# Batches 0 and 1 combined, and two groups' attention scores begun, beside the rear expert tiles

## The chip, the cores and the metric

The kernel runs on one NeuronCore of one Trainium2 chip, in fp32 throughout. The metric is the device time of one execution in microseconds; the median of three runs is given. Engines are named as in the profile: PE (TensorE), PEld (its weight loads), DVE (VectorE), ACT (ScalarE), POOL (GpSimd), SP (SyncE, which only issues DMAs here).

## The reference, cut to what matters

Four batches (B) of 512 tokens (S) with 256 features (D) go through four blocks. Each block adds its output to x.

```python
x = x + L0_xattn(layernorm(x), ctx, ctx)       # attention over log-ratios, then an MLP of 1024
x = x + L0_ffn(layernorm(x))                   # 8 experts of 1024, every token goes to its best two
x = x + L1_xattn(layernorm(x), ctx, ctx)       # 16 heads of 16 features
x = x + L1_ffn(x)                              # 8 experts of 512, every token goes to its best one

# L0_ffn, for all tokens t = (x @ W_in + b_in) of all four batches:
probs = softmax(t @ W_gate + b_gate);  topv, topi = top_k(probs, 2);  topv /= sum(topv)
out = (sum over the two: topv * (relu(t @ W1[e] + b1[e]) @ W2[e] + b2[e])) @ W_out + b_out

# L1_xattn, per batch and head:
scores = (q @ k.T) / sqrt(16);  ctx = softmax(scores) @ v;  out = ctx @ Wo + bo

# L1_ffn: one expert per token
out = max(gates) * (gelu(x @ W1[e] + b1[e]) @ W2[e] + b2[e])
```

## The kernel before, in words

**Layer 0, dense part.** Attention and MLP of the four batches run interleaved. `choose` picks each token's two experts and `Dispatch.send` scatters the token's row, with its share and its number, into an array `sent` in DRAM, where each expert has a region of its own. Keys and values of layer 1 need only the context; `remember` computes them here and stores them to DRAM.

**Layer 0, expert tiles.** A tile is 256 rows of one expert (TT). Which expert and which row a tile has is known only on the chip. `leave` and `plan` compute it on DVE in small operations (8 to 184 elements per partition) from the counts of rows; SP reads expert and row with `value_load`. One tile, of the expert with most rows, is worked early inside the dense part (`work`). Then `Dispatch.tiles` runs 19 tiles (`usual`) without a branch, and behind a branch on the true count (L625, L626) the few that may be left, which these inputs do not need.

One tile is: `load` (rows from `sent`, w1, w2, b1, b2 by SP), `turned` (4 transposes, `psIn`), `hide` (8 chunks of `mid` with their PSUM tiles `pm`, evicted by ACT and DVE in turn, L638 and L636), `give` (2 tiles `po`; ACT makes y = b2*share at L598, DVE adds po*share at L601) and `scatter` (POOL writes y's rows to `came` by an indirect DMA, L523). The next tile's `load` and `turned` stand between a tile's `hide` and its `give`. In layer 1 (`direct`) a tile has 4 chunks, x is gathered by POOL (L506), DVE adds it at L605, and POOL scatters to the output.

**The order of tiles.** The tiles that hold batch 0's rows come first: `send.zero` keeps the counts after batch 0, and `leave` makes from it how many tiles of each expert stand in front (`front`). After at most 11 tiles (FRONT) batch 0 is complete in `came`. So `bring(0, ..)` loads its two picks, `combine(0)` adds them and multiplies by W_out (L1105), `prepare(0)` normalizes and makes the queries `qc` (L1125), in steps of three after each tile, by `also(i)`. `place(0)` copies the queries by 16 small DMAs of SP into `qT`, where each head has 32 partitions. `early` clears `kT`, `qT` and `va` on POOL (`places`) and fetches batch 0's keys and values.

**Layer 1, attention.** A group is four heads of one batch; there are 16 groups. Scores are made twice: by query (`sc`, for the row maximum, DVE reduces it into `nm` at L1218) and by key (`scT`, ACT takes the exponential at L1215). `put_greatest` transposes `nm` and adds the negated maximum into row 0 of each head in `qT`. Scores by query run two groups ahead (AHEAD = 2), so the loop starts at group -2: groups -2 and -1 only have scores by query, four heads at a time. Later a quartet is two `sc` and two `scT` on four row groups of PE. `weigh` multiplies with the values (`av`, L1232), `divide` normalizes. Between quartets, two lanes (`fore`, `back_`) fill in the combining and preparing of batches 1 to 3, `finish` and `choose`. PE's order is written by hand here; in the expert tiles all engines' orders come from the framework's planner.

```python
            fore.work += [waiting(4), combines[1], prepares[1], placed(1), prepares[2], prepares[3]]
            back_.work += [waiting(5), combines[2], waiting(6), combines[3]]
            for i in range(-AHEAD, groups):
```

**Layer 1, expert tiles.** Three tiles are worked early (`work`, `soon`), then 8 tiles by `tiles`.

Of the kernel before, what the change touches and what calls it, by code (L numbers as in the profile page):

```python
# [43 lines left out]
def xattn_ffn_kernel(ctx: ExitStack, tc: tile.TileContext, a: dict, out: bass.AP):  # L44
# [240 lines left out]
    class Dispatch:  # L285


        def __init__(self, layer, pool, seen, n, func, b1_all):
            self.layer, self.pool, self.group = layer, pool, f"send{layer}"
            self.n, self.func, self.b1_all = n, func, b1_all  # L290
            self.w1_all, self.w2_all, self.b2_all = (a[f"L{layer}_ffn_{x}"] for x in ("W1", "W2", "b2"))
            self.kept = []
            self.zero = None
            self.seen_pool = seen
            self.seen = seen.tile([P, NT + 1, NE], F32, tag="seen0", name="seen0")
            nc.vector.memset(self.seen[:, 0, :], 0.0)
# [82 lines left out]
        def leave(self):  # L379
# [13 lines left out]

            front = least
            past_used = small.tile([P, NE, CAP // TT], F32, tag="past_used", name="past_used", bufs=1)
            nc.vector.tensor_tensor(past_used, over(used, CAP // TT), full, ALU.add)
            if self.zero is not None:
                more = small.tile([P, NE, CAP // TT], F32, tag="more", name="more", bufs=1)
                front = small.tile([P, NE], F32, tag="front", name="front")
                nc.vector.tensor_tensor(more, over(self.zero, CAP // TT), past_used, ALU.is_gt)  # L400
                nc.vector.tensor_reduce(front, more, AX.X, ALU.add)
                nc.vector.tensor_tensor(front, front, least, ALU.max)

            behind = small.tile([P, NE + 1], F32, tag="behind", name="behind")
            nc.vector.memset(behind[:, NE : NE + 1], float(NE * CAP))
            nc.vector.scalar_tensor_tensor(behind[:, 0:NE], front, float(TT), start[:, 0:NE], ALU.mult, ALU.add)
            nc.vector.tensor_copy(start[:, NE : NE + 1], behind[:, 0:1])
            self.stride = pool.tile([P, NE], F32, tag="stride", name="stride")
            nc.vector.tensor_tensor(self.stride, behind[:, 1 : NE + 1], behind[:, 0:NE], ALU.subtract)
            self.full = pool.tile([P, NE, CAP // TT], F32, tag="full_i", name="full_i")  # L410
            nc.vector.scalar_tensor_tensor(
                self.full, over(front, CAP // TT), float(TT), past_used, ALU.mult, ALU.add
            )

            self.first = pool.tile([P, TILES0], F32, tag="first_i", name="first_i")
            if self.zero is not None:
                end = small.tile([P, NE], F32, tag="end", name="end")
                nc.vector.tensor_tensor_scan(end, ones[:, 0:NE], front, 0.0, ALU.mult, ALU.add)
                jump = small.tile([P, NE], F32, tag="jump", name="jump")
                nc.vector.tensor_tensor(jump, start[:, 1 : NE + 1], start[:, 0:NE], ALU.subtract)  # L420
                nc.vector.scalar_tensor_tensor(jump, front, -float(TT), jump, ALU.mult, ALU.add)
                past = small.tile([P, TILES0, NE], F32, tag="past", name="past", bufs=1)
                nc.vector.tensor_tensor(past, number, end.unsqueeze(1).to_broadcast([P, TILES0, NE]), ALU.is_ge)
                self.e_front = pool.tile([P, TILES0], F32, tag="e_front", name="e_front")
                nc.vector.tensor_reduce(self.e_front, past, AX.X, ALU.add)
                nc.vector.scalar_tensor_tensor(
                    self.e_front, self.e_front, float(NE), self.e_front, ALU.is_lt, ALU.mult
                )
                nc.vector.tensor_tensor(past, past, jump.unsqueeze(1).to_broadcast([P, TILES0, NE]), ALU.mult)
                nc.vector.tensor_reduce(self.first, past, AX.X, ALU.add)  # L430
                nc.vector.scalar_tensor_tensor(
                    self.first, number[:, :, 0], float(TT), self.first, ALU.mult, ALU.add
                )
                nc.vector.tensor_scalar(self.first, self.first, start[:, 0:1], None, ALU.add)
                self.in_front = pool.tile([P, 1], F32, tag="in_front", name="in_front")
                nc.vector.tensor_copy(self.in_front, end[:, NE - 1 : NE])
            else:
                nc.vector.tensor_scalar(self.first, number[:, :, 0], float(TT), start[:, 0:1], ALU.mult, ALU.add)

            self.row_0 = pool.tile([P, 1], I32, tag="row_0", name="row_0")  # L440
            nc.vector.tensor_copy(self.row_0, start[:, 0:1])

        def plan(self):
# [11 lines left out]
            nc.vector.tensor_scalar(end, end, 1.0 if self.zero is None else self.in_front, None, ALU.add)  # L455
# [13 lines left out]
            if self.zero is None:  # L469
# [93 lines left out]
        def tiles(self, n_tiles, usual, tp, midp, pm_pool, po_pool, also):  # L563
# [30 lines left out]
            def give(rows, w2, added, mid):  # L594
                b2, x = added
                y = tp.tile([P, TT // P, D], F32, tag="y", name="y", bufs=2 if x is None else 3)
                for u in range(TT // P):
                    nc.scalar.mul(y[:, u, :], b2, rows[:, u, D:TO])  # L598

                def take(u, po):  # L600
                    nc.vector.scalar_tensor_tensor(  # L601
                        y[:, u, :], po, rows[:, u, D:TO], y[:, u, :], ALU.mult, ALU.add
                    )
                    if x is not None:
                        nc.vector.tensor_tensor(y[:, u, :], y[:, u, :], x[:, u, :], ALU.add)  # L605
                    self.scatter(rows, u, y)

                together(project(mid, w2, po_pool, take))

            def run(first, last):  # L610
# [3 lines left out]
                for i in range(first, last):  # L614
                    mid = midp.tile([P, n // P, TT], F32, tag="mid", name="mid")
                    together(hide(mid, w1, inT, b1, self.func, pm_pool))
# [4 lines left out]
                    give(*now)  # L621
                    also(i)

            run(0, usual)
# [53 lines left out]
    with tc.tile_pool(name="l0a", bufs=2) as lp, tc.tile_pool(name="l0tmp", bufs=2) as tp, tc.tile_pool(  # L678
# [279 lines left out]
        for b in range(B):  # L958
# [9 lines left out]
            if b < B - 1:  # L968
# [3 lines left out]
                if b == 1:  # L972
                    n, _ = send.counted("n0")
                    send.zero = fp0.tile([P, NE], F32, tag="zero", name="zero")
                    nc.vector.tensor_copy(send.zero, n[:, 0, :])
# [12 lines left out]
            with tc.manual_schedule(engines={mybir.EngineType.PE}):  # L988
# [24 lines left out]
                together(second)  # L1013
                send.plan()
# [12 lines left out]
    for i in range(2):  # L1027
        nms.append(heads.tile([P, NT, 4, 32], F32, tag=f"nm{i}", name="nm"))
        nc.gpsimd.memset(nms[i], 0.0)

    def places(pool):
# [3 lines left out]
        qT = pool.tile([P, NG, S], F32, tag=f"qT{i}", name=f"qT{i}")  # L1035
        va = pool.tile([P, NT, HEADS, 32], F32, tag=f"va{i}", name=f"va{i}")
        kTs.append(kT)
        qTs.append(qT)
        vas.append(va)
        for w in (kT, qT, va):  # L1040
            tc.keep_in_program_order(nc.gpsimd.memset(w, 0.0))
            yield
# [40 lines left out]
    def bring(b, k, pool, engine):  # L1083

        if b not in ys:
            tag = f"y{b}" if b == 0 else "w1" if b % 2 else "w2"
# [22 lines left out]
    def prepare(b, pool):  # L1109
# [4 lines left out]
        qc = qcs[b] = pool.tile([P, NC, S], F32, tag="qc", name="qc", bufs=1 if b == 0 else 2)  # L1114
# [15 lines left out]
    def place(b):  # L1130

        qT = qTs[b % 2]
        if b:
            together(fetch(b))
        if b > 1:
            for r in range(4):
                nc.gpsimd.memset(qT[32 * r : 32 * r + 1, :, :], 0.0)
        for hd in range(HEADS):
            g, r = divmod(hd, 4)
            m, at = divmod(hd * DH, P)  # L1140
            tc.keep_in_program_order(
                nc.sync.dma_start(qT[32 * r + 1 : 32 * r + 1 + DH, g, :], qcs[b][at : at + DH, m, :])
            )
# [3 lines left out]
    FRONT = (2 * S + NE * (TT - 1)) // TT  # L1147
# [35 lines left out]
    with tc.tile_pool(name="l1a", bufs=2) as lp, tc.tile_pool(name="l1s", bufs=1) as sp, tc.tile_pool(  # L1183
# [149 lines left out]
        def waiting(n):  # L1333
            yield n
# [182 lines left out]
```

## Time and profile before

| | us |
|---|---|
| median of 3 runs (1004.81 to 1006.11) | 1006.1 |
| the profiled execution | 1005.28 |
| its span, first to last instruction | 1003.5 |
| PE busy | 950.3 |
| DVE busy | 518.5 |
| ACT busy | 362.4 |
| POOL busy | 291.4 |
| mean granted TensorE clock | 0.987 |

Places in the span: the 19 tiles of layer 0 take PE from 303.65 to 585.05, the first mixed quartet of the attention starts at 612.65, and layer 1's 8 tiles take PE from 930.3 to 993.2.

How to read it: lines give start and length in us, the engine, the line of the kernel, the operation with its result and operands, and in square brackets how long the engine was idle before and what ended that. A matmul of fp32 appears as two records. A time given from one start to the next is more telling than a record's own length, since matmuls overlap. L12 is line 12 of the kernel before.

### The profile page before, as it was taken

Reading aid. Unit: us, or ns where it says so; the run is one execution under the profiler, and the core shown is the slowest. Engines: PE = TensorE matmul, PEld = TensorE weight load, DVE = VectorE, ACT = ScalarE, POOL = GpSimd, SP = SyncE. Lnnn points to the kernel's source line nnn. Section 1 sums busy time; section 2 is a strip of 40 time slices with the busy share of each in tenths; the row PEclk is TensorE's granted clock in tenths of the full one; section 3 lists DMA queues with packets and bytes.
Section 4 is the critical chain, followed back from the end, with each engine's and each line's share of the span. In section 5 each row is a group of like instructions: output and inputs, shape, how many; then the busy total and the mean of one; then the engine's idle time right before and its main releaser. Section 6 shows DMA issues by size and latency. Waiting matters only on the chain. (4 is left out here: it accounts for less than half of the span.)

```text
span 1003.5 us, 14228 instructions
## 1 busy us (share of the span) xinstructions
PE 950.3 (95%) x4885; PEld 640.2 (64%) x4885; DVE 518.5 (52%) x1401; ACT 362.4 (36%) x703; POOL 291.4 (29%) x333
## 2 busy tenths in 40 slices
PE   6999899899999999999999989999999999997995
PEld 4656667575778888888888854333333433356784
DVE  6674665566752222222323258576687777724232
ACT  5654232213212111211121204655656555573331
POOL 4341233244241312211112155315023221133453
PEclk9999999999999999999999999999999999999998
DMA  8599999944244566557654441101011103045672
GB/s 278 195 257 250 247 243 241 243 118 153 86 143 142 187 216 209 174 179 259 233 160 161 130 148 33 27 12 47 2 38 48 43 1 105 32 115 154 211 225 73
DMA packets 113233, 146.05 MB, mean 146 GB/s; under 512 B 14580, under 2 KB 94717, under 8 KB 113152
## 3 DMA queue, kind: packets, MB, share of 16 engines
q1 hardware_dynamic: 106112, 128.19, 45.3%
q0 software_dynamic: 6624, 15.80, 4.8%
q8 instruction: 43, 0.70, 0.3%
q10 hardware_dynamic: 416, 1.05, 0.3%
q14 instruction: 38, 0.31, 0.1%
HBM read 86.71 MB, written 58.80 MB: 145 GB/s over the span
## 5 line engine op out<-in xcount | busy, mean ns | idle before, releaser
L1218 DVE TENSOR_REDUCE nm<-sc 128x1 f32<-128x512 f32 x256 | 165.2, 683 | 60.9 <-PE scT L1211 57.3
L1215 ACT ACTIVATE ex<-scT 128x512 f32<-128x512 f32 x256 | 138.4, 596 | 96.2 <-PE scT L1211 95.8
L634 PE MATMUL pm<-inT,w 128*128 128x256 f32 x736 | 166.3, 382 | 2.5 <-ACT mid L638 2.1
L647 PE MATMUL po<-w,mid 128*128 128x256 f32 x736 | 163.3, 379 | 0.0
L1211 PE MATMUL sc<-kT,qT 32*128 32x512 f32 x512 | 154.5, 650 | 3.7 <-DVEq L626 1.6
L634 PEld LDWEIGHTS pm<-inT,w 128*128 128x128 f32 x736 | 139.9, 191 | 23.6 <-ACT mid L638 4.0
L647 PEld LDWEIGHTS po<-w,mid 128*128 128x128 f32 x736 | 138.1, 190 | 17.8
L1211 PE MATMUL scT<-qT,kT 32*128 32x512 f32 x512 | 148.5, 639 | 0.9 <-ACT ex L1215 0.9
L523 POOL DMA_INDIRECT came<-y,rows x38 | 37.4, 985 | 224.1 <-DVE y L601 224.1
L244 POOL TENSOR_TENSOR rstd<-var,halved 128x4 f32<-128x4 f32 (+1 forms) x32 | 28.1, 882 | 228.9 <-DVE var L243 224.4
L601 DVE SCALAR_TENSOR_TENSOR y<-po,rows,y 128x256 f32<-128x256 f32 x54 | 26.1, 484 | 130.5 <-PE po L647 120.6
L638 ACT ACTIVATE mid<-pm,b 128x256 f32<-128x256 f32 x108 | 49.9, 471 | 109.2 <-PE pm L634 93.5
L1211 PEld LDWEIGHTS sc<-kT,qT 32*128 32x128 f32 x512 | 49.8, 185 | 59.9 <-DVE nm L1218 36.9
L636 DVE TENSOR_SCALAR mid<-pm,b 128x256 f32<-128x256 f32 x76 | 36.7, 483 | 95.0 <-PE pm L634 95.0
L598 ACT ACTIVATE y<-b,rows 128x256 f32<-128x256 f32 x54 | 24.5, 500 | 159.2 <-DMA b<-in_L_ffn_b 133.0
L339 POOL DMA_INDIRECT sent<-rows,slot x48 | 47.3, 985 | 102.8 <-DVE slot L336 62.3
L1232 PE MATMUL av<-ex,va 128*32 128x512 f32 x512 | 68.6, 605 | 0.0
L763 PE MATMUL pm<-hT,w 128*128 128x512 f32 x128 | 62.2, 611 | 0.5 <-DVE hT L676 0.5
L769 PE MATMUL po<-w,mid 128*128 128x256 f32 x256 | 59.2, 381 | 0.0
L769 PEld LDWEIGHTS po<-w,mid 128*128 128x128 f32 x256 | 47.9, 190 | 9.1 <-issue 3.1
L1211 PEld LDWEIGHTS scT<-qT,kT 32*128 32x128 f32 x512 | 45.6, 183 | 6.0 <-issue 4.2
L1232 PEld LDWEIGHTS av<-ex,va 128*32 128x32 f32 x512 | 10.2, 108 | 48.2 <-issue 36.4
(312 smaller groups left out, 1257.6 us busy)
## 6 DMA issues: line engine op xcount, KB each, us to landing
w<-in_L_ffn_W SPq DMA_DIRECT2D x40, 1024.0 KB, 7.2
sent<-nowhere SPq DMA_DIRECT2D x32, 1161.0 KB, 20.4
w<-in_L_ffn_W SPq DMA_DIRECT2D x22, 512.0 KB, 4.3
rows<-sent SPq DMA_DIRECT2D x27, 258.0 KB, 4.9
b<-in_L_ffn_b SPq DMA_DIRECT2D x28, 128.0 KB, 6.6
y<-came SPq DMA_DIRECT2D x6, 512.0 KB, 8.7
x<-in_x SPq DMA_DIRECT2D x4, 512.0 KB, 5.1
c<-in_ctx SPq DMA_DIRECT2D x4, 512.0 KB, 5.6
```

The costliest lines, as they stand in the source:

```text
L339: i = nc.gpsimd.indirect_dma_start(out=sent[self.layer][:, :], out_offset=bass.IndirectOffsetOnAxis(ap=slot[:, t - tts[0], k : k + 1], axi ...
L523: i = nc.gpsimd.indirect_dma_start(out=came[self.layer][:, :], out_offset=bass.IndirectOffsetOnAxis(ap=rows[:, u, TO:ROW].bitcast(I32), ax ...
L634: nc.tensor.matmul(pm, w1[:, c, ts(k, P)], inT[:, c, :], start=c == 0, stop=c == NC - 1)
L636: nc.vector.tensor_scalar(mid[:, k, :], pm, bias[:, k : k + 1], 0.0, ALU.add, ALU.max)
L638: nc.scalar.activation(mid[:, k, :], pm, func, bias=bias[:, k : k + 1])
L647: nc.tensor.matmul(po, mid[:, k, ts(t, P)], w2[:, k, :], start=k == 0, stop=k == n - 1)
L763: nc.tensor.matmul(pm, w1_mlp[:, c, ts(k, P)], hT[:, c, :], start=c == 0, stop=c == NC - 1)
L769: nc.tensor.matmul(po, mid[:, k, ts(t, P)], w2_mlp[:, k, :], start=k == 0, stop=k == HD // P - 1)
L1211: nc.tensor.matmul(sc, stay, move, start=True, stop=True)
L1215: nc.scalar.activation(ex, sc, AF.Exp, scale=1.0 / DH**0.5)
L1218: nc.vector.tensor_reduce(nm[:, t, head, 0:1], sc, AX.X, ALU.max, negate=True)
L1232: nc.tensor.matmul(av[32 * head : 32 * head + 32, :], vas[b % 2][:, t, 4 * g + head, :], exs.pop((t, head)), start=t == 0, stop=t == NT - 1,)
```

## The change

- `leave` keeps only what the first tile needs. A new `fronts` makes the fronts for a list of counts (`until`: after batch 0, and after batches 0 and 1), so that batch 0's tiles come first, then the rest of batch 1's, then the others. For layer 0 it is called before `plan`, for layer 1 straight after `leave`.
- FRONT is now a list, 11 and 15 tiles. `also` brings batch 0 at tiles 10 and 11 and batch 1 at 14 and 15, and combines and prepares each in two portions (7 steps, then the rest), two and three tiles later.
- `between(i, k)` is called after each step of `hide` and `project`. From tile 14 it issues batch 0's 16 query copies, on POOL and ACT in turn. In the last three tiles, after every second step, it makes a pair of scores by query (two heads of one row tile) of groups 0 and 1, 16 pairs in all, in the PSUM buffers that `hide` or `give` doesn't use at that time; after the eighth pair `put_greatest(0)`.
- The attention's loop starts at group 0. Batch 1's combine and prepare are gone from its lanes; its queries are copied at the end of the tiles, its keys and values fetched at the attention's start. `qT` and `nm` of both batches are cleared with the first `places`.
- In layer 1's tiles y is made by two operations of DVE (po*share + x, then + b2*share) instead of one on ACT and two on DVE.
- The planned tiles of both layers run with SP in source order.

```diff
+        def fronts(self):
+            pool, here, past_used = self.pool, self.start, self.past_used
+            self.first = pool.tile([P, TILES0], F32, tag="first_i", name="first_i")
+            nc.vector.tensor_scalar(self.first, number[:, :, 0], float(TT), here[:, 0:1], ALU.mult, ALU.add)
+            ahead, before_ = None, least
+            for n in self.until:
...
             def give(rows, w2, added, mid):
                 b2, x = added
                 y = tp.tile([P, TT // P, D], F32, tag="y", name="y", bufs=2 if x is None else 3)
-                for u in range(TT // P):
-                    nc.scalar.mul(y[:, u, :], b2, rows[:, u, D:TO])
+                if x is None:
+                    for u in range(TT // P):
+                        nc.scalar.mul(y[:, u, :], b2, rows[:, u, D:TO])
                 def take(u, po):
-                    nc.vector.scalar_tensor_tensor(
-                        y[:, u, :], po, rows[:, u, D:TO], y[:, u, :], ALU.mult, ALU.add
-                    )
-                    if x is not None:
-                        nc.vector.tensor_tensor(y[:, u, :], y[:, u, :], x[:, u, :], ALU.add)
+                    share = rows[:, u, D:TO]
+                    if x is None:
+                        nc.vector.scalar_tensor_tensor(y[:, u, :], po, share, y[:, u, :], ALU.mult, ALU.add)
+                    else:
+                        nc.vector.scalar_tensor_tensor(y[:, u, :], po, share, x[:, u, :], ALU.mult, ALU.add)
+                        nc.vector.scalar_tensor_tensor(y[:, u, :], b2, share, y[:, u, :], ALU.mult, ALU.add)
                     self.scatter(rows, u, y)
...
-                    together(hide(mid, w1, inT, b1, self.func, pm_pool))
+                    for k, _ in enumerate(hide(mid, w1, inT, b1, self.func, pm_pool)):
+                        if between and i < usual:
+                            between(i, k)
...
-            run(0, usual)
+            with tc.manual_schedule(engines={mybir.EngineType.SP}):
+                run(0, usual)
...
-                if b == 1:
+                if b in (1, 2):
                     n, _ = send.counted("n0")
-                    send.zero = fp0.tile([P, NE], F32, tag="zero", name="zero")
-                    nc.vector.tensor_copy(send.zero, n[:, 0, :])
+                    send.until.append(fp0.tile([P, NE], F32, tag=f"until{b}", name=f"until{b}"))
+                    nc.vector.tensor_copy(send.until[-1], n[:, 0, :])
...
                 together(second)
+                send.fronts()
                 send.plan()
...
+    def by_query(i, t, heads_, pool, tag):
+        b, g = divmod(i, NG)
+        made = []
+        for head in heads_:
+            r = slice(32 * head, 32 * head + 32)
+            made.append(pool.tile([P, S], F32, tag=tag, name="sc"))
+            nc.tensor.matmul(made[-1], qTs[b % 2][r, g, ts(t, P)], kTs[b % 2][r, g, :], start=True, stop=True)
+        for head, sc in zip(heads_, made):
+            nc.vector.tensor_reduce(nms[i % 2][:, t, head, 0:1], sc, AX.X, ALU.max, negate=True)
...
-    FRONT = (2 * S + NE * (TT - 1)) // TT
+    FRONT = [(2 * n * S + NE * (TT - 1)) // TT for n in (1, 2)]
...
+        moved, leads = queries(0, [nc.gpsimd, nc.scalar]), lead()
+        def between(i, k):
+            if i > FRONT[0] + 2:
+                next(moved, None)
+            if i >= usual - 3 and k % 2:
+                try:
+                    leads.send((po_pool, "po") if k < HD // P else (pm_pool, "pm"))
+                except StopIteration:
+                    pass
         def also(i):
             next(early, None)
+            for b in range(2):
+                n = i + 1 - FRONT[b]
+                if 0 <= n < 2:
+                    bring(b, n, tp, nc.gpsimd)
+                elif n == 2:
+                    together(part(batches[b], STEPS))
+                elif n == 3:
+                    together(batches[b])
+            if i + 1 == usual:
+                together(early)
+                together(moved)
+                together(queries(1, [nc.sync]))
...
-            fore.work += [waiting(4), combines[1], prepares[1], placed(1), prepares[2], prepares[3]]
-            back_.work += [waiting(5), combines[2], waiting(6), combines[3]]
+            fore.work += [waiting(5), combines[2], prepares[2], prepares[3]]
+            back_.work += [waiting(13), combines[3]]
-            for i in range(-AHEAD, groups):
+            for i in range(groups):
```

## The prediction

> **What bounds the kernel now.** I read the page first (busy shares and slices), then the table of stretches, then the timeline of the two places that the change touches, then the groups kept apart by shape.
>
> ```profile
> PE 950.3 (95%) x4885; PEld 640.2 (64%) x4885; DVE 518.5 (52%) x1401; ACT 362.4 (36%) x703; POOL 291.4 (29%) x333
> PE   6999899899999999999999989999999999997995
> DVE  6674665566752222222323258576687777724232
> ```
>
> TensorE bounds nearly all of it. Only its idle time, and matmul time that can be taken off it, are worth anything. The other engines have room in the expert tiles (DVE at 2 tenths there). The table of stretches gives the expert tiles of layer 0, the passage from them into the attention of layer 1, that attention's first two groups, and the expert tiles of layer 1 (columns: length, then busy time with the number of instructions for PE, PEld, DVE, ACT, POOL; clock; DMA share; GB/s):
>
> ```profile
> 303.65:585.05 281.40, 280.57 (x1333) 245.74 (x1332) 72.62 (x149) 55.86 (x120) 55.47 (x53) 1.00 0.55 180
> 585.05:612.65 27.60, 23.60 (x100) 12.63 (x100) 24.05 (x46) 3.15 (x5) 20.55 (x13) 0.94 0.46 157
> 612.65:652.31 39.66, 38.79 (x245) 15.64 (x245) 25.45 (x51) 23.15 (x44) 13.03 (x12) 1.00 0.08 18
> 930.30:993.20 62.90, 60.38 (x289) 51.45 (x287) 19.93 (x40) 18.83 (x44) 29.90 (x30) 1.00 0.64 189
> ```
>
> The reader sees that layer 0's tiles leave PE 0.8 us idle in 281, so whatever is put beside them is paid in full on PE. In the passage PE looks busy for 23.6 of 27.6 us, but DVE is the one that is full (24.05): these are the 32 row maxima of groups 0 and 1, 683 ns each, 21.9 us. The PE timeline of the passage:
>
> ```profile
> 577.98 7.07 PE L647 MATMUL po<-w,mid 128*128 128x256 f32 x32
> 586.67 1.22 PE L1211 MATMUL sc<-kT,qT 32*128 32x512 f32 x5 [1.62 <-DVEq L626]
> 588.77 9.79 PE L1211 MATMUL sc<-kT,qT 32*128 32x512 f32 x35 [0.89 <-issue]
> 603.87 1.09 PE L1075 MATMUL psTr<-ident,y 128*128 128x128 f32 x8
> 605.21 2.05 PE L1105 MATMUL po<-L_ffn_W_out,aT 128*128 128x256 f32 x8 [0.24 <-ACT aT L1076]
> ```
>
> The tiles' last matmul ends at 585.05 and the first mixed quartet starts at 612.65. The third place is the start and run of layer 1's expert tiles:
>
> ```profile
> 925.15 0.91 ACT L598 ACTIVATE y<-b,rows 128x256 f32<-128x256 f32 x2 [3.27 <-DMA rows<-sent]
> 925.96 0.45 ACT L638 ACTIVATE mid_t<-pm,b_s 128x256 f32<-128x256 f32 x1
> 926.47 4.07 PE L647 MATMUL po<-w,mid_t 128*128 128x256 f32 x10 [2.95 <-ACT mid_t L638]
> 941.57 0.91 ACT L598 ACTIVATE y<-b,rows 128x256 f32<-128x256 f32 x2 [5.54 <-DMA b<-in_L_ffn_b]
> 942.38 1.18 ACT L638 ACTIVATE mid<-pm,b 128x256 f32<-128x256 f32 x3
> 942.89 1.13 PE L634 MATMUL pm<-inT,w 128*128 128x256 f32 x4 [1.32 <-ACT mid L638]
> ```
>
> ACT's y = b2*share (L598) waits for a DMA at the head of ACT's queue. The PSUM evictions of `mid` stand behind it, and PE behind those.
>
> **The change, part by part.** All sums are PE time on the path.
>
> *1. Layer 0's rear tiles take more.* Batch 1's combine costs what batch 0's costs there: two groups of transposes of 0.44 us (503.99 to 504.43) and 16 records of 0.216 (32 in 6.9 us), 4.3. Its prepare is the same work by count, 4.3. `put_greatest(0)` is 0.5. New are 16 pairs of scores. A quartet of four row groups takes 1.07 us now (two rounds of 0.54: 613.19 to 613.73), and one matmul alone takes 0.42 for a round (647.08 to 647.50). So a pair streams for 0.86 to 1.07. A filler of four records in a quartet's company takes 1.06 against 0.86 in the tiles, so going into 32-row work and back costs 0.2. A pair is 1.06 to 1.27; I take 1.17: 18.7 (17.0 to 20.3). [...] Sum of part 1: 27.8.
>
> *2. The passage goes.* 27.6 us fall away, except the branch at L626 and the gap after it (1.62 + 0.89), which stay: -25.1.
>
> *3. The first groups of the attention.* Group 0 lasts from 612.65 to 634.43. Batch 1's prepare leaves it and group 1: two transposes of 0.58 and four pieces of 1.06, 5.4, with the 0.9 us stall at 616.9 that its normalization on ACT makes. Batch 2's transposes, made in the passage now, come in: +1.2. Part of the filler was free: a cycle of two quartets and one `av` needs 2*1.07+1.0 = 3.1 of PE, yet takes 3.96 with no filler (645.11 to 649.07), because PSUM's six buffers come back at the pace of evictions. I take back 1.3. Sum: -3.8 (-2.5 to -5.5).
>
> *4. ACT's L598 goes in layer 1.* At 922 to 926 the third early tile loses 2.95 us and its slowed matmuls (4.07 for 10 records instead of 2.2) as well. Its last matmul would end near 925.9, and the rows of the first tile landed at 925.15; tile 0 can begin 4.2 us earlier (930.33 to about 926.1). Inside the tiles the waits for ACT of 1.32, 0.42, 0.30 and 0.40 go: 2.4. What is late next: b2's buffer is now freed by DVE's last operation of a tile, some 1.1 us after PE's end, instead of by ACT's early one. Behind b2 in SP's queue stand w1, w2 and the next rows. w1 is then issued about 1.7 us after a tile's end, lands 3.9 to 4.7 us later (the DMA view of this stretch), and is due 7.3 us after that end: 1 us to spare. I charge 0.2; the bound is 8 tiles at 0.5. DVE exchanges a tensor_tensor of 424 ns for an operation of 484: 0.06 at the very end. Sum: -6.3 (-2.5 to -7).
>
> *5. `fronts()`.* About 33 small DVE operations (0.15 to 0.35 us each, some 7 us) replace about 16, and stand in source just ahead of plan() instead of at 248. Their inputs are ready from 250 on, and DVE has gaps then. If they fill those: 0. If all of them come after 285, the second tile's expert and row come some 4 us late, behind a plan that ends at 291 and is read near 297; SP then holds that tile's rows and weights: up to +3. I take +0.7.
>
> *6. Queues passed.* SP in source order: in the trace SP issues rows, w1, w2, b1, b2 per tile in layer 0 and rows, b1, b2, w1, w2 in layer 1, which is source order already: 0 (-1 to +1). The 16 copies of batch 1's queries (10.7 us of SP now) come behind the last tile's load, with a tile of 20 us to hide in; SP must be through before the branch. Batch 0's 16 copies go to POOL and ACT, 8 each, at 0.6 us on POOL (its direct DMA) and 0.4 on ACT. The memsets of qT1 and nm, 1.8 and 0.5 us, move into the first two tiles; two more loads of `came` wait on POOL. All that POOL does can hold up this chain:
>
> ```profile
> 319.67 0.98 POOL L523 DMA_INDIRECT came<-y,rows  x1 [2.48 <-DVE y L601]
> 322.30 0.39 SPq L500 DMA_DIRECT2D rows<-sent  x1
> 325.55 0.60 PE L519 MATMUL psIn<-ident,rows 128*128 128x128 f32 x4
> ```
>
> The scatter of one tile frees the rows buffer of the next but one, and those rows land just when PE needs them (no slack in a plain tile). The memsets follow the scatter now and have 10 us there; in the rear tiles the pairs lengthen PE's side by 4.7 us. I set 0 (to +3). The 0.82 us that PE waits at 539 for batch 0's normalization goes, since that work gets a tile of lead; I set against it 0.8 for batch 1's add on POOL (2.35 us) and for row maxima ahead of evictions on DVE. Batch 2's add now precedes its first transpose by less: POOL is free for it about 9 us into the attention, PE wants it at about 14; +0.5 (0 to +4). The early load of the exponential's table is at most 1.28 us of an ACT that is busy 56 of 281 us: 0.
>
> Sum: 27.8 - 25.1 - 3.8 - 6.3 + 0.7 + 0.5 = -6.2 us. The profiled execution took 1005.28 (span 1003.5 and 1.8 around it), so 999.1; the median of the runs shown is 0.8 above it, so I say 999.9.
>
> **The rivals.**
> [...]
> - *Layer 1's tiles give it back.* If w1 lands late behind b2, or the DMA share there (0.64, up to 0.81) slows it, part 4 falls to -2.5 and the kernel takes 1003.7.
> [...]
> - *It doesn't do what it says*: nothing is removed from PE but order (rear tiles +27.8 against -25.1 - 3.8), parts 5 and 6 are paid, and part 4's stalls are replaced by others: 1006.2.
>
> **How the numbers follow.** Forecast (996 to 1003) 0.52, giving back part (1003 to 1004) 0.11, more than forecast 0.10, no change 0.08, slower by the pairs or another of the charged waits 0.19. What a measurement of this kernel can tell from no change is about 0.2%, 2 us. So faster 0.73, same 0.08, slower 0.19. The range from 993.5 to 1008 leaves out about 0.06 below and 0.12 above.
>
> **What would show it.** In the profile after: no L598 rows in layer 1 and PE without waits for ACT between 920 and the end; last matmul of layer 0's tiles near 612, first mixed quartet 2.5 us behind it; group 0 in about 15 us instead of 21.8; pairs followed by a tile matmul 1.1 to 1.2 us later. I am wrong if a pair takes over 1.5 us, if PE waits in plain tiles for `rows` after a scatter, if SP or POOL holds the branch, or if layer 1's tiles wait for weights.

## The result, and the profile after

The changed kernel takes 1016.0 us (median of 13 runs, 1011.0 to 1019.6), the kernel before 1007.1 us beside it (13 runs, 1001.6 to 1015.6): the ratio is 1.0068, with a 95% interval of 1.0042 to 1.0094. It is slower, by 9 us between the medians and by 7 us by the ratio, where 6 us less were forecast, and lies outside the forecast's range. The profiled execution took 1019.52 us, with a span of 1017.7; it is one of the longest of the 13. Line numbers in each view are those of its own kernel: L511 of the changed kernel is L496 of the kernel before.

The head of the page of the changed kernel (busy time, slices of PE, granted clock by slices):

```profile
PE 963.0 (95%) x4887; PEld 638.1 (63%) x4887; DVE 524.0 (51%) x1420; ACT 356.7 (35%) x687; POOL 295.5 (29%) x343
PE   5899999999987999999999998999999999999996
PEclk9999999999997999999999998999999998999999
```

PE has 12.7 us more of busy time with two instructions more. So matmuls became slower or overlap less: the clock row has a 7 and two 8s, and the one of before has none of these until its last slice. The first is near 310 us, the others near 620 to 635 and 850. (The clock row gives the share of full speed that was granted to TensorE; "half clock" below is a granted clock of 0.50.) The table of stretches, cut at the early tile's last matmul, the first loop tile's first, the last matmul of layer 0, `psCtx` of group 0 (the transposes of its result), the last `av` and the last matmul:

```profile
302.42:313.32 10.90, 1.74 (x6) 1.00 (x6) 1.18 (x2) 0.91 (x2) 0.99 (x1) 0.68 0.47 142
313.32:624.55 311.23, 310.70 (x1450) 257.04 (x1450) 97.41 (x196) 62.73 (x134) 69.31 (x69) 0.99 0.51 168
624.55:657.00 32.45, 28.85 (x161) 10.03 (x162) 17.52 (x30) 13.56 (x25) 17.95 (x15) 0.89 0.34 105
657.00:914.24 257.24, 253.54 (x1694) 97.52 (x1693) 175.80 (x399) 147.27 (x277) 64.02 (x60) 0.98 0.13 40
914.24:1007.95 93.71, 90.66 (x450) 78.01 (x450) 37.78 (x106) 27.59 (x53) 43.01 (x43) 1.00 0.64 185
```

The same cuts in the kernel before last 5.08, 281.40, 58.20, 249.53 and 100.42 us. So the reader sees a new gap of 5.8 us ahead of the tiles, 29.8 more in them, 18.0 less in passage and attention together, and 6.7 less at the end.

**The gap ahead of the tiles** (timeline):

```profile
303.22 0.99 POOL L538 DMA_INDIRECT came<-mid_s,rows_s  x1 [2.46 <-DVE mid_s L560]
305.91 0.35 SPq L511 DMA_DIRECT2D b<-in_b_col  x1
306.94 2.19 SPq L515 DMA_DIRECT2D rows<-sent  x2
311.40 1.74 PE L534 MATMUL psIn<-ident,rows 128*128 128x128 f32 x6 [8.98 <-DMA rows<-sent]
```

SP issues the first load of the loop's tiles after the early tile's scatter has landed: of SP's waits in this stretch (line, what it waited for, us in total, times, longest) one is

```profile
SPq L511 <- DMA came<-mid_s,rows_s: 7.1, 1, 7.1
```

The kernel before has no such wait. There the load was issued 3 us before the early tile ended at 298.57:

```profile
295.54 0.35 SPq L496 DMA_DIRECT2D b<-in_b_col  x1
302.10 1.63 PE L519 MATMUL psIn<-ident,rows 128*128 128x128 f32 x8 [3.53 <-DMA rows<-sent]
```

PE idles 8.98 us instead of 3.53.

**The pairs beside the rear tiles** lie as planned, one after each eight matmuls, and PE waits for no row maximum:

```profile
554.43 1.13 PE L1181 MATMUL sc<-kT,qT 32*128 32x512 f32 x4
555.49 1.99 PE L658 MATMUL pm<-inT,w 128*128 128x256 f32 x8
557.42 1.13 PE L1181 MATMUL sc<-kT,qT 32*128 32x512 f32 x4
```

From start to start a pair is 1.06, and the eight records behind it take 1.93 instead of the 1.73 of eight in a row: 1.26 a pair.

**The start of the attention** (timeline, ACT's first exponential and PE around it):

```profile
625.82 0.66 PE L1293 MATMUL sc<-kT,qT 32*128 32x512 f32 x1 [1.27 <-DVEq L650]
630.51 1.57 ACT L1297 ACTIVATE ex<-scT 128x512 f32<-128x512 f32 x3 [14.47 <-DMA came<-y,rows]
631.16 2.07 PE L1293 MATMUL scT<-qT,kT 32*128 32x512 f32 x2 [2.33 <-ACT ex L1297]
634.20 1.22 PE L1293 MATMUL sc<-kT,qT 32*128 32x512 f32 x1
636.22 1.60 PE L1306 MATMUL av<-ex,va 128*32 128x512 f32 x8
637.75 0.69 PE L1293 MATMUL sc<-kT,qT 32*128 32x512 f32 x1
```

The passage is gone, as forecast. But the first exponential waits for the last tile's scatter to land, and for what POOL does behind it: the scatter's packets have moved by 627.4, and POOL then has one more instruction of the branch at L650, which ends at 629.8, 0.7 us ahead of the exponential (line, instruction, count: least, median and greatest ns, first and last start):

```profile
L650 POOLq EVENT_SEMAPHORE  x4: 17/43/1735, 625.9 to 627.9; - x4
L650 POOLq INC_SWDGE_SEM  x1: 1861/1861/1861, 628.0 to 628.0; - x1
```

PSUM's six buffers are full by then, and PE stops for 2.33 us. Behind it a record takes 1.22 instead of 0.69 and an `av` 1.60 instead of 1.06: half the clock, for some 6 us.

The kernel before had half clock behind its branch too, from 589.17 to 592.58:

```profile
589.17:592.58 3.41, 3.41 (x16) 2.04 (x11) 2.56 (x5) 0.00 (x0) 2.13 (x2) 0.50 0.35 103
```

It is in the clock of 0.94 that the passage's row showed. There DVE, full with row maxima (24.05 of the 27.6 us), set the pace of the passage; how much of the half clock showed in the time was not traced.

**The later dip**, in the changed kernel:

```profile
852.12 0.98 PE L1293 MATMUL sc<-kT,qT 32*128 32x512 f32 x1 [1.02 <-DVE nm L1300]
855.77 1.22 PE L1293 MATMUL sc<-kT,qT 32*128 32x512 f32 x1
861.07 0.69 PE L1293 MATMUL sc<-kT,qT 32*128 32x512 f32 x1
```

and at the same instruction in the kernel before:

```profile
835.19 0.69 PE L1211 MATMUL sc<-kT,qT 32*128 32x512 f32 x1 [1.02 <-DVE nm L1218]
```

The wait of 1.02 us is the same in both; only one of them is followed by half the clock. The two profiles differ in where the clock changes. In both profiles, changes between full and half lie on one grid: the changed kernel has them at 306.27, 630.53, 852.40 and 883.12, which are 95, 65 and 9 steps of 3.413 us apart, and the kernel before at 302.45, 589.17 and 927.09, 84 and 99 such steps. Cut along this grid (columns as above, the clock third from the end), first the changed kernel, then the kernel before:

```profile
848.99:852.40 3.41, 2.24 (x14) 0.99 (x12) 3.20 (x16) 1.68 (x3) 0.24 (x2) 1.00 0.11 39
852.40:859.23 6.83, 6.83 (x28) 1.85 (x30) 3.51 (x7) 1.68 (x3) 0.00 (x0) 0.50 0.38 132
831.52:834.93 3.41, 2.51 (x16) 0.72 (x8) 3.10 (x18) 2.06 (x4) 0.42 (x2) 1.00 0.11 39
834.93:838.34 3.41, 3.15 (x21) 0.80 (x21) 2.59 (x5) 0.60 (x1) 0.00 (x0) 1.00 0.00 0
```

PE has two idle times here in every version, 0.15 and 1.02 us, some 1.1 us apart. In the changed kernel both lie inside one step, which leaves PE 1.17 us idle in it, and the next step is at half clock. In the kernel before a step ends within the second one, at 834.93.

**Layer 1's tiles** have no `y` on ACT any more; the third early tile's `po` runs through without the 2.95 us, and what is left are short waits for rows:

```profile
943.51 3.62 PE L671 MATMUL po<-w,mid_t 128*128 128x256 f32 x16
947.90 0.63 PE L534 MATMUL psIn<-ident,rows 128*128 128x128 f32 x4 [0.33 <-DMA rows<-sent]
```

### The profile page after: what moved, and what is told of

Its sections match the earlier page's. It is cut to its first block, busy times and chain, and to the rows that moved or that the text cites. A ratio compares the mean times of both kernels' runs of the same rounds, so it can differ in the third digit from the quotient of the medians.

```text
span 1017.7 us, 14220 instructions
## 1 busy us (share of the span) xinstructions
PE 963.0 (95%) x4887; PEld 638.1 (63%) x4887; DVE 524.0 (51%) x1420; ACT 356.7 (35%) x687; POOL 295.5 (29%) x343
## 5 line engine op out<-in xcount | busy, mean ns | idle before, releaser
L1300 DVE TENSOR_REDUCE nm<-sc 128x1 f32<-128x512 f32 x224 | 145.6, 683 | 65.1 <-PE scT L1293 64.6
L658 PE MATMUL pm<-inT,w 128*128 128x256 f32 x736 | 168.6, 383 | 0.4 <-DVE inT L535 0.2
L1293 PE MATMUL scT<-qT,kT 32*128 32x512 f32 x512 | 155.6, 655 | 2.3 <-ACT ex L1297 2.3
L1293 PE MATMUL sc<-kT,qT 32*128 32x512 f32 x448 | 144.2, 654 | 2.5 <-DVEq L650 1.3
L1293 PEld LDWEIGHTS sc<-kT,qT 32*128 32x128 f32 x448 | 43.4, 188 | 55.1 <-DVE nm L1300 35.6
L619 DVE SCALAR_TENSOR_TENSOR y<-po,rows,y 128x256 f32<-128x256 f32 x38 | 18.4, 484 | 106.0 <-PE po L671 95.1
L614 ACT ACTIVATE y<-b,rows 128x256 f32<-128x256 f32 x38 | 17.2, 500 | 128.5 <-DMA b<-in_L_ffn_b 91.0
```

The source lines that it names most:

```text
L658: nc.tensor.matmul(pm, w1[:, c, ts(k, P)], inT[:, c, :], start=c == 0, stop=c == NC - 1)
L1293: nc.tensor.matmul(sc, stay, move, start=True, stop=True)
L1300: nc.vector.tensor_reduce(nm[:, t, head, 0:1], sc, AX.X, ALU.max, negate=True)
```

## The experiments

Theory: the forecast's terms on PE are about right, and two waits on scatters, which the layout of SBUF makes, with the clock behind them, take more than the gain. In the two programs, the work pool of layer 0's tiles ends at byte 182,752 of a partition before and at 211,328 after; the early tile's `mid_s` begins at 205,088 and 204,992. The loaded tiles (`b1`, `rows`) share no byte with `mid_s` in either. For the second wait: the attention's pool that holds `ex` begins at 170,208 in the changed program, inside the work pool and 160 bytes before the end of its second `y` buffer. Rivals: SP's source order or a late plan delays the first loads; the pairs or the attention are dearer than forecast. Ratios are to the kernel before, run beside each kernel. The kernels of sp_order_only, pool_reaches, add_on_dve and bias_on_dve ran on a chip on which the kernel before took 1018.0 us and the first 200 us moved 222 to 235 GB/s where the profile before has 244 and 245; their times are compared only by ratio.

**y_once**

```diff
-            ys[b] = pool.tile([P, 2, NT, D], F32, tag=tag, name=f"y{b}")
+            ys[b] = pool.tile([P, 2, NT, D], F32, tag=tag, name=f"y{b}", bufs=1 if b < 2 else 2)
```

The pool gives two buffers to each tag, so that y0 and y1 hold 16 KB each and use half of it. Now the pool ends at 194,944.

> The changed kernel with bufs=1 for y0 and y1: the work pool of layer 0's tiles ends below the early tile's `mid_s`, so SP's first loads need not wait for that tile's scatter. Theory (the new layout's wait costs 5.8 us at the start of the loop of tiles): b1 is issued before the early tile ends, the gap from the early tile's last matmul to the first loop tile goes from 10.9 to about 5 us (perhaps 0.5 more, since the first eviction to `mid` now waits for that scatter), and the time is some 5.5 us below the changed kernel: ratio to the kernel before about 1.001. Rival (the later first loads come from SP's source order or from a late plan): the gap stays near 11 us and the ratio near 1.007.

Measured: 1009.0 us, ratio 1.0016 (0.9987 to 1.0045). The timeline:

```profile
297.19 0.35 SPq L511 DMA_DIRECT2D b<-in_b_col  x1
301.91 0.99 POOL L538 DMA_INDIRECT came<-mid_s,rows_s  x1 [2.46 <-DMA rows<-sent]
305.41 8.13 PE L658 MATMUL pm<-inT,w 128*128 128x256 f32 x32
```

SP's load comes 4.7 us ahead of the scatter, and the gap is 4.3 us instead of 10.9. The median fell by 7 us, by the ratios 5 (a difference of 0.0052, some 0.004 either way as estimated from the two intervals). `rows` and `b1` have the same addresses as in the changed kernel; only what lies behind them in the pool, and so its extent, differs. With the plan and SP's order unchanged, both rivals for this wait fall.

**pool_reaches**

```diff
+        tp.tile([P, 5760], F32, tag="apart", name="apart", bufs=1)
         send.tiles(TILES0, usual, tp, midp, pm_pool, po_pool, also)
```

> The kernel before with nothing but 22.5 KB a partition of unused room at the end of the work pool of layer 0's tiles, so that the pool reaches over the early tile's `mid_s`, as it does in the changed kernel. Theory (the pool's extent, not any use of the same bytes by the loaded tiles, makes SP's first load wait for the early tile's scatter): b1 is issued some 3 us after the early tile's end instead of before it, the gap ahead of the first loop tile goes from 5 to about 11 us, ratio 1.005 to 1.006. Rival (the wait is one of the changed kernel's other edits): gap 5 us, ratio 1.000.

Measured: ratio 1.013 (1.0072 to 1.0187).

```profile
309.17 0.99 POOL L523 DMA_INDIRECT came<-mid_s,rows_s  x1 [2.45 <-DVE mid_s L545]
316.74 0.36 SPq L496 DMA_DIRECT2D b<-in_b_col  x1
323.22 1.94 PE L519 MATMUL psIn<-ident,rows 128*128 128x128 f32 x8 [14.85 <-DMA rows<-sent]
```

Unused room, and nothing else in the source, puts SP's first load behind the scatter in time; the rival's 5 us did not come. But the gap is 16.8 us (3.1 in sp_order_only) where 11 were expected, and the scatter does not account for it. Its packets had moved by 311.1, 1.9 us after POOL's issue began, as in the changed kernel (305.2, issue at 303.22). Until 316.1 SP was reading experts and rows of 13 tiles into its registers; the kernel before reads only 4 experts and 3 rows ahead of its first load (its experts are the third line):

```profile
L483 SPq TENSOR_LOAD <-expert_i x13: 262/271/274, 299.1 to 315.0; - x13
L484 SPq TENSOR_LOAD <-row_i x13: 265/268/472, 301.2 to 315.6; - x13
L483 SPq TENSOR_LOAD <-expert_i x4: 262/266/272, 289.3 to 294.5; - x4
```

SP's order is the planner's here, and source order in the changed kernel, so the room changed that order too. It also stands at the pool's start and not at its end: the loaded tiles begin 23,040 bytes higher, and the pool ends at 205,792. So this run does not show the changed kernel's wait by itself; y_once does.

**sp_order_only**

```diff
-            run(0, usual)
+            with tc.manual_schedule(engines={mybir.EngineType.SP}):
+                run(0, usual)
```

> The kernel before with SyncE in source order in the planned tiles and nothing else. Theory: its loads are in that order already, so 0 (ratio 0.998 to 1.002), the gap ahead of the first loop tile stays near 5 us. Rival (the order is what makes the first loads late in the changed kernel): that gap near 11 us, ratio 1.006.

Measured: ratio 1.0002 (0.9974 to 1.003), gap 3.1 us. SP's order costs nothing and gains nothing, as forecast.

**exp_apart**: y_once, and

```diff
-    with tc.tile_pool(name="l1a", bufs=2) as lp, tc.tile_pool(name="l1s", bufs=1) as sp, tc.tile_pool(
+    with tc.tile_pool(name="l1s", bufs=1) as sp, tc.tile_pool(name="l1a", bufs=2) as lp, tc.tile_pool(
+        sp.tile([P, 64], F32, tag="apart", name="apart")
```

> As y_once, and the attention's pools opened in the other order with 256 bytes of padding, so that `ex` lies beyond the memory that layer 0's last scatter reads. Theory (the first exponential waits for a scatter that the prologue used to cover): ACT's first exponential starts about 2.5 us after the last tile matmul instead of 6, TensorE's stall of 2.33 us and the half clock behind it go, 5 to 6 us below y_once, ratio about 0.995. Rival (the exponentials wait for something else, and the clock falls there anyway): within 1 us of y_once.

Measured: 1006.0 us, ratio 0.9982 (0.9952 to 1.0013).

```profile
617.52 1.08 ACT L1298 ACTIVATE ex<-scT 128x512 f32<-128x512 f32 x2 [11.00 <-PE scT L1294]
618.79 1.22 PE L1294 MATMUL scT<-qT,kT 32*128 32x512 f32 x1 [0.52 <-issue]
```

The exponential comes 2.5 us after the last tile matmul, and PE's stall is 0.52 instead of 2.33. The half clock came all the same, at 618.79. So `psCtx` of group 0 gained 2.2 us (30.0 after the last tile matmul, 32.2 in y_once), not 5 to 6: the theory held for the stall and failed for the clock. The medians differ by 3 us, with intervals that overlap, so the gain itself is not clear of the noise.

**no_branch**: exp_apart, and

```diff
-            total = nc.values_load(self.total[0:1, 0:1], min_val=0, max_val=TILES0)
-            with tc.If(total > usual):
-                run(usual, n_tiles)
+            if direct:
+                ...
```

> exp_apart without layer 0's branch to tiles past the planned number; this leaves out the tiles that another input could need. Theory (TensorE's idle time at the branch, 1.3 us, and the next short one are what sets off the half clock that cost the first scores and `av` of the attention some 3 us in exp_apart): both go, 4 us below exp_apart, ratio 0.994. Rival (the clock falls there or elsewhere in any case): 1.3 us below exp_apart, ratio 0.997, with records of 1.22 us somewhere in the first 20 us of the attention.

Measured: 1001.6 us, ratio 0.9948 (0.9923 to 0.9972), 4.4 us below exp_apart by the medians and 3.4 by the ratios, whose intervals overlap. Against y_once the gain is clear of the noise. The clock row of its page, the stretch up to `psCtx` of group 0, and PE's first quartet:

```profile
PEclk9999999999999999999999999999999999999999
```

```profile
614.37:641.53 27.16, 24.71 (x161) 8.65 (x160) 17.43 (x30) 13.59 (x25) 18.00 (x15) 1.00 0.40 125
```

```profile
615.02 0.69 PE L1295 MATMUL sc<-kT,qT 32*128 32x512 f32 x1 [0.65 <-DVE y L619]
```

The idle time ahead of the first quartet is 0.65 instead of 1.26, and there is no record of 1.22 us: psCtx comes after 27.2 instead of 30.0. The theory for the start holds in this profile. That the dip near 850 is missing too is not explained by the branch: a step of the clock's grid ends at 835.16 here, between the two idle times, of which the longer begins at 835.79.

**l1_tiles_only**: the kernel before with the changed `give`,

```diff
-                for u in range(TT // P):
-                    nc.scalar.mul(y[:, u, :], b2, rows[:, u, D:TO])
+                if x is None:
+                    for u in range(TT // P):
+                        nc.scalar.mul(y[:, u, :], b2, rows[:, u, D:TO])
...
+                        nc.vector.scalar_tensor_tensor(y[:, u, :], po, share, x[:, u, :], ALU.mult, ALU.add)
+                        nc.vector.scalar_tensor_tensor(y[:, u, :], b2, share, y[:, u, :], ALU.mult, ALU.add)
```

> The kernel before with one part of the change alone: in layer 1's tiles b2*share moves from ACT to DVE. Theory: as in the changed kernel, 6.7 us from the end of the attention to the last matmul, ratio 0.9935. Rival (those 6.7 us come in part from the other timing of the changed kernel's end): 0.997.

Measured: ratio 0.9951 (0.9927 to 0.9975). In its profile the end, from the last `av` to the last matmul, takes 93.0 us instead of 100.4. Yet its attention, line by line that of the kernel before, took 314.7 us instead of 307.7: half the clock at 604 to 611 and again in the three groups that last 20.9, 20.1 and 20.1 us instead of 18.6, 19.4 and 18.7. Such dips belong to the execution and not to the change. In the twelve profiles the dip near 850 follows the clock's grid without exception. In eight (the changed kernel, y_once, exp_apart, l1_tiles_only, sp_order_only, add_on_dve, bias_on_dve, pool_add_first) the idle times of 0.15 and 1.02 us lie in one step, and half clock follows. In the other four a step ends within the second (the kernel before, quartets, pool_reaches) or between the two (no_branch), and it does not.

**quartets**: exp_apart, and the scores beside the rear tiles four heads at a time,

```diff
-                    for pair in range(2):
-                        pool, tag = yield
-                        by_query(i, t, (2 * pair, 2 * pair + 1), pool, tag)
+                    spare, busy = yield
+                    by_query(i, t, range(4), [busy, spare, spare, spare])
...
-            if i >= usual - 3 and k % 2:
+            if i >= usual - 3 and k % 4 == 1:
```

> As exp_apart, and the 16 pairs of scores beside the rear tiles made as 8 quartets of four row groups (three PSUM tiles from the pool that rests, one from the busy one). Theory (a round of two costs nearly what a round of four costs, 1.06 us, plus 0.2 for the change to and from 32-row work): 8*1.27 = 10.2 instead of 20.2 us, ratio about 0.985. Rival (four row maxima of 0.68 us in a row on DVE hold PSUM and the evictions of `mid`, or four 32-row matmuls cost twice two): no gain against exp_apart, or a loss.

Measured: 1002.4 us, ratio 0.9956 (0.9935 to 0.9977), where 0.985 was expected; the interval overlaps that of exp_apart. Layer 0's tiles take 306.4 us instead of 311.6.

```profile
552.00 1.14 PE L1181 MATMUL sc<-kT,qT 32*128 32x512 f32 x8
553.08 1.99 PE L658 MATMUL pm<-inT,w 128*128 128x256 f32 x8
560.02 0.51 ACT L614 ACTIVATE y<-b,rows 128x256 f32<-128x256 f32 x1 [8.30 <-DMA b<-in_L_ffn_b]
560.94 1.13 PE L671 MATMUL po<-w,mid 128*128 128x256 f32 x4 [2.84 <-ACT mid L662]
629.44 4.64 POOL L1120 TENSOR_TENSOR y<-y 128x1024 f32<-128x1024 f32 x2
631.83 1.12 PE L1102 MATMUL psTr<-ident,y 128*128 128x128 f32 x4 [3.64 <-POOL y L1120]
```

Eight records on four row groups take 1.08 from start to start, as long as the four of a pair (1.06). So eight quartets for 16 pairs save the expected 10 us on PE. Half of it goes to two waits, 2.84 for an eviction that stands behind ACT's `y` (and that behind a load of b2), and 1.41 for a row maximum. The rival held for that half, with ACT beside DVE. In the attention a wait that the changed kernel had covered comes up: PE waits 3.64 us for batch 2's add, which stands on POOL behind 11 us of memsets, and those behind the last scatter.

**add_on_dve**: quartets, and

```diff
-        (nc.gpsimd if b else nc.vector).tensor_tensor(y[:, 0, :, :], y[:, 0, :, :], y[:, 1, :, :], ALU.add)
+        (nc.gpsimd if b % 2 else nc.vector).tensor_tensor(y[:, 0, :, :], y[:, 0, :, :], y[:, 1, :, :], ALU.add)
```

> As quartets, and batch 2's first add of the attention goes to DVE instead of POOL. In quartets TensorE waited 3.64 us for that add, which stood behind 11 us of memsets on POOL, and ran at half clock for some 5 us behind it. Theory (this wait took the place of the exponentials' wait): the stall and the half clock go, group 0's `psCtx` comes 26 to 28 us after the last tile matmul instead of 32.5, 5 us below quartets, ratio 0.991. Rival (DVE's row maxima wait behind the add and TensorE waits for them instead): within 1 us of quartets.

Measured: ratio 0.9978 (0.9959 to 0.9998); `psCtx` of group 0 comes 34.4 us after the last tile matmul.

```profile
628.88 1.23 DVE L1120 TENSOR_TENSOR y<-y 128x1024 f32<-128x1024 f32 x1 [6.24 <-DMA y<-came]
630.76 1.21 PE L1294 MATMUL sc<-kT,qT 32*128 32x512 f32 x1 [5.38 <-DVE nm L1301]
```

The theory fell, and its rival held: the ratio is not below that of quartets (the intervals overlap). DVE waits 6.24 us for the load of `came`, with a row maximum behind it, and PE waits 5.38 for that. The same wait on POOL had nothing urgent behind it.

**bias_on_dve**: add_on_dve, and in layer 0's tiles

```diff
-                if x is None:
-                    for u in range(TT // P):
-                        nc.scalar.mul(y[:, u, :], b2, rows[:, u, D:TO])
...
+                        nc.vector.tensor_scalar(y[:, u, :], po, share, None, ALU.mult)
...
+                    nc.vector.scalar_tensor_tensor(y[:, u, :], b2, share, y[:, u, :], ALU.mult, ALU.add)
```

> As add_on_dve, and b2*share moves from ACT to DVE in layer 0's tiles too. In quartets TensorE waited 2.84 us for an eviction of `mid` that stood behind b2*share on ACT, which waited for the load of b2. Theory: those 2.8 us and some of the 1.4 us of another wait go, about 3.5 us below add_on_dve, ratio 0.9875. Rival (DVE, which also makes the row maxima and half of the evictions, gives it back): not below add_on_dve.

Measured: ratio 1.0 (0.9973 to 1.0028), where 0.9875 was expected: as the rival said, it is not below add_on_dve. The loss is not in the tiles of layer 0, which take 303.8 us instead of 306.6, near what was expected. The wait for the add, which stands on DVE here too, has grown to 6.39 us, and its half clock comes with it: `psCtx` after 36.9 us.

**pool_add_first**: bias_on_dve with the add on POOL again, and POOL's other work split around it,

```diff
-            together(places(sp))
-            together(fetch(1))
+            last = [places(sp), fetch(1)]
+            together(part(last[0], 2))
+            together(part(last[1], NG + 1))
...
+                    if n == 6 and i == 0:
+                        together(last[0])
+                        together(last[1])
```

> Quartets, with b2*share on DVE in layer 0's tiles, and on POOL batch 2's add ahead of 7.3 us of memsets and of batch 1's copies of values. Theory: layer 0's tiles take 304 us as in bias_on_dve (306.4 in quartets), TensorE's wait of 3.64 us for POOL's add shrinks to about 1 (the load of `came` lands some 11 us after the last tile) and with it the half clock behind it, psCtx of group 0 comes 27 to 29 us after the last tile matmul: 6 us below quartets, ratio 0.990. Rival (another wait comes in its place, such as the load of `came` itself): 2.5 us below quartets, 0.993.

Measured: 996.3 us (6 runs), ratio 0.9887 (0.9848 to 0.9927). The tiles take 303.7 us, PE no longer waits for the add, and `psCtx` of group 0 comes after 29.7 us. It is the best of the versions and faster than both kernels, though its profile still has half the clock at 612 to 618 and in the last groups.

## Why the prediction was wrong, point by point

Lengths in the profiles, less those of the kernel before, beside the forecast (us):

| | forecast | after | y_once | exp_apart | no_branch |
|---|---|---|---|---|---|
| early tile's end | 0 | +3.9 | +2.5 | 0.0 | +0.2 |
| gap to the first loop tile | +0.7 | +5.8 | -0.8 | -0.2 | -0.9 |
| layer 0's loop tiles | +27.8 | +29.8 | +29.2 | +30.2 | +30.0 |
| passage and attention | -28.4 | -18.0 | -18.4 | -20.6 | -26.4 |
| end of attention to the last matmul | -6.3 | -6.7 | -7.2 | -6.4 | -7.8 |
| sum | -6.2 | +14.8 | +5.3 | +2.9 | -4.9 |

Most of the first row is not the change: up to 220 us PE runs the same instructions in the same order in both kernels, and is 2.8 us late there already.

Two steps of the forecast failed, and both hold a wait behind a scatter that it put at nothing: the end of the passage (2) and the first loads of the tiles (6). By the ratios of the runs, y_once takes back 5 us, and exp_apart and no_branch together 7 more (1.0068, 1.0016, 0.9948), each sum clear of the noise.

1. *Rear tiles (part 1)*: right in kind, 2.0 us short. A pair is 1.26 and not 1.17, which makes 1.4 of it, and half clock at the loop's start, up to 316.51 here and 305.86 before, makes 0.5. Two row groups take 1.06 here and four 1.08 in quartets, so a quartet does the work of two pairs in the time of one. No run shows by itself what going into 32-row work and back costs, which the forecast put at 0.2: the runs show 1.93 instead of 1.73 for the eight records behind a pair, and not the cause.
2. *The passage goes (part 2)*: a step that failed. PE's and DVE's time in it was right. But 26 us were taken out between the last scatter and the first exponential, and I did not ask what they covered: a wait for that scatter, and for POOL's part of the branch behind it (1.9 us), in memory that `ex` takes over, and half clock behind the branch, which the passage's own row showed as 0.94. The wait costs 2.3 us and the half clock, in the executions profiled, some 3 (worked out for exp_apart: 2.8 more than no_branch up to `psCtx`, of which 1.1 are idle time, while no_branch waits 1.5 longer for POOL). Both go in no_branch. It is 2.0 us above the forecast all the same, though it lacks 1.9 of the 2.5 us at the branch that the forecast kept. Of these 3.9, POOL's add makes 1.3 (1.8 where 0.5 was charged) and half clock near 866 another 1.3 (a group of 20.0 us instead of 18.7); the rest was not traced.
3. *First groups, and batch 2's add (parts 3 and 6)*: the add was charged 0.5, with 0 to 4 as bounds. In the changed kernel the other stalls cover it, and when they go it is 1.8 (no_branch) to 3.6 us (quartets).
4. *Layer 1's tiles (part 4)*: right: -6.7 here, -7.4 alone. b2's later release, charged 0.2, does not show.
5. *`fronts()` (part 5)*: no cost. The plan's end leaves SP free to issue at 297.19 in y_once.
6. *Queues passed (part 6)*: the other step that failed. SP's order is 0, as forecast. What was missed is not in a queue's order but in memory: the second pair of batch buffers made the work pool longer, and SP's first load came behind a scatter. That is the 5.8 us of the gap, where the forecast had 0.7 for a late plan; undoing it (y_once) shows it.

Of the 21 us between forecast and profile, 5.1 are this gap, 10.4 the attention, 3.9 the early part, 2.0 the tiles, and the end gave 0.4 back. The attention's 10.4 hold 2.3 of stall, some 3 of half clock behind it, and 4.2 of the later dip (groups of 21.3, 19.8 and 20.0 us against 18.8, 19.4 and 18.7 in quartets); 0.9 are left over. That dip and most of the early part lie in the profiled execution, by luck of where the clock's grid fell and of the first 60 us: the medians differ by 9 us, not 14. The forecast had 0.19 for a slower kernel, by the pairs or another of the charged waits; it was not the pairs, at 1.26 us each, and no rival had a wait from memory in it. Why half clock then lasts one step in some profiles (3.41 us from 589.17 in the kernel before) and two in others (6.83 from 630.53 in the changed kernel) stays open.

## What to carry to other kernels

Before a stretch is taken out, list what runs under it (a scatter still landing, a load, memsets on POOL) and who reads or reuses its memory next, since each can become a wait at the new seam (2.33 us of PE here, 3.64 in quartets). A change that adds a buffer moves every pool behind it: compare where pools end and begin in both programs, because the first use of a pool can wait for the last user of a neighbour with which its tiles share no byte (SP's first load waited 7.1 us for the early tile's scatter in the changed kernel; in y_once it came 4.7 us ahead of that scatter). A run that only pads memory can still change the planner's order, as pool_reaches did, so its order is compared before its time is. And a wait is moved to another engine only after asking what stands behind it there: DVE waited 6.24 us for the load of `came` in add_on_dve and PE 5.38 for the row maximum behind it, where POOL had nothing urgent behind the same wait.

## What the runs showed of the hardware

- The granted clock of TensorE changed between 1.00 and 0.50 on a grid of 3.413 us, whose place differs from execution to execution (changes at 306.27, 630.53 and 852.40 in the changed kernel, at 302.45, 589.17 and 927.09 in the kernel before). Half clock came after steps with 1.17 us of idle time (the changed kernel at 852.40, and seven other profiles at the same place) and 1.41 us (exp_apart at 618.81), and lasted 6.8 us in both. These profiles give no threshold of idle time: a step with 1.9 us of it, in the gap ahead of the tiles, was followed by full clock (bias_on_dve, the step that ends at 311.18), and one without idle time to speak of (0.1 us), among scores by query alone, was followed by half (l1_tiles_only at 604.00).
- Two 32-row matmuls side by side took as long as four (1.06 us in the changed kernel at 554.43 and 1.08 in quartets at 552.00, for 512 columns).
- The packets of an indirect scatter of 128 rows moved 1.5 to 1.9 us after POOL's issue began (the changed kernel: issue at 303.22, packets from 304.75 to 305.15; pool_reaches: issue at 309.17, packets from 310.7 to 311.1).
